# A cross-attention block on one core: V chains and encoder rows moved between units, a layer norm ahead of a V chain, and the last residual rows behind the last exchange

## The chip, the core and the metric

The kernel runs on one core of a Trainium2 chip. A core has TensorE (matmuls; the profile calls it PE, and its weight loads PEld), VectorE (DVE), ScalarE (ACT), GpSimd (POOL) and SyncE (SP), which here only issues transfers (DMAs). Each engine works through its own instructions in order, and waits for others by semaphores. The metric is the time of one execution on the device in microseconds (us); less is better. Everything is float32.

## What is computed

For each of four batches, with 512 query rows `x` and 512 encoder rows, 16 heads of 32 and a hidden width of 2048:

```python
residual = hidden_states
x = layer_norm(hidden_states, ln1_w, ln1_b)
q = (x @ q_w + q_b)      # then split into 16 heads
k = (encoder_hidden_states @ k_w + k_b)
v = (encoder_hidden_states @ v_w + v_b)
scores = jnp.einsum('bhqd,bhkd->bhqk', q, k) * scale
scores = jnp.where(mask, scores, mask_value)
attn = jax.nn.softmax(scores, axis=-1)
out = jnp.einsum('bhqk,bhkd->bhqd', attn, v)
hidden = out @ cproj_w + cproj_b + residual
y = layer_norm(hidden, ln2_w, ln2_b)
y = jax.nn.gelu(y @ fc_w + fc_b, approximate=True)
return hidden + y @ proj_w + proj_b
```

## The kernel before

**Groups and units.** The 16 heads of a batch are cut into four groups of four heads (128 columns), so that there are 16 groups `w` in all, four for each batch. A group has four units, one for each tile of 128 query rows. Unit `u = 4 w + qt` runs from 0 to 63. The texts call the columns of group `w` "K w", "Q w" and "V w": three chains of matmuls, `prep_k` (L230), `prep_q` (L240) and `prep_v` (L251). K and V read the batch's encoder rows `eT`, Q reads the normalized and transposed rows `xT`; both lie in one buffer, `xe`, one batch at a time. When a chain is done, ACT takes it out of PSUM, and the weights of two groups on (`load_w(w + 2)`) are loaded into the place of the weights just used. V's bias is added by POOL (`v_bias`, L267).

**One unit** is the loop body near L876. `scores` (L272): four matmuls into one PSUM tile with four banks (one buffer, so the next unit's scores wait until DVE has read it); for each head DVE adds the mask and takes the minimum (L284), ACT takes the exponential and its sum (L288). `turn` (L292): DVE transposes 32 by 32 blocks (L302) into a buffer `tb` that two units share. After the second, the reciprocals of the sums are added (L307 to L311), and a **pair** is formed: pair `p = 2 w + half`, formed in unit `2 p + 1`. `exchange` and `copies` (L320, L331) then move the pair's blocks between partitions with 16 DMAs (L345) of 136 KB on SP's queue. Pairs 1, 3, 5 and 7 go to `gt`, pairs 25 to 31 (odd ones) to `xe`, the others to the one buffer `pT`, which must have been read before.

**The attend.** `attend` (L348) multiplies a pair's blocks with V (32 matmuls, L362), and DVE scales the result into `oT` (L367). It stands at the head of a unit, before that unit's scores. Which unit is told by the table `AT` (L66) and, for units that aren't in it, by the rule "unit minus `LAG` (4), halved": pair 7 is attended in unit 18 before the change, pair 6 in 17, pair 8 in 20, pair 29 in 63.

**What else a unit does** is written by hand in the lists `first[w]` and `later[w]` (L790 to L866). A tuple in `first[w]` names the work of each of the four units; a list is spread over them by costs (`CHAIN` 3.4 and so on). This work follows the unit's scores and turn. It holds the chains of later groups (`A(w)`), the inputs of the next batch (`inputs(b)`: load of `x`; `x2`, the layer norm's two statistics parts and its application; `x3`, four turns by TensorE of that norm into `xT`; `x4`, the load of the encoder rows), output chains (`C(b)`, `cproj`, L399), and parts of the MLP (`some(n)` takes the next n of `mlp`). Layer norm 2 of a batch is `stat` (DVE, L145 and L146), `rs` (POOL, L151 and L153), `norm` (DVE, L167), and `turns2` (four turns by TensorE, L176, taken out by ACT and DVE, L181 and L179). `proj_bias` and `c_bias` add a row to four tiles on POOL (L374). All small accumulators share a ring of four PSUM banks (`ps_acc`), in order of use.

**The end.** For the last batch, `load_h` (L380) loads `x` again as the residual into places of K and Q that are free by then, and `c_bias` adds the output bias; `cproj` of that batch needs them, after the last attend. After the loop come the rest of the MLP's first part, the two last attends, the last output chains and `last_mlps`.

All these loads and exchanges go through SP's queue, in the order in which the program issues them.

Of the kernel before, what the change touches and what calls it, by code (L numbers as in the profile page):

```python
# [46 lines left out]
B, L, D, H = 4, 512, 512, 16  # L47
HD = D // H
INNER = 4 * D
NT = L // P  # L50
# [12 lines left out]
IN_G = (1, 3, 5, 7)  # L63
IN_XE = (25, 27, 29, 31)

AT = {u: (u - 5) // 2 for u in (5, 7, 9, 11, 13, 15, 17, 53, 55, 57, 59, 61, 63)}  # L66
BY_ACT = ((1, 1),)
MW = 8
WARM = 9
# [8 lines left out]
def xattn_block(ctx: ExitStack, tc: tile.TileContext, x, encT, mask, q_w, k_w, v_w, c_w, fc_w, p_w, vecs, rows, out):  # L78
# [36 lines left out]
    def k_q(w, i):  # L115
        n = w % 4 * 2 + i
        return pbt[:, n * D : (n + 1) * D]
# [19 lines left out]
    def acc_tile(name):  # L137
        return ps_acc.tile([P, D], F32, tag="acc", name=name)
# [9 lines left out]
    def ln_rs(key):  # L148

        ve = small.tile([P, NT], F32, tag="ve", name=f"ve{key[0]}_{key[1]}")  # L150
        nc.gpsimd.tensor_scalar(ve, S["mv", key][:, :, 1], EPS, 1.0, ALU.add, ALU.mult)  # L151
        rs = small.tile([P, NT], F32, tag="rs", name=f"rs{key[0]}_{key[1]}")
        nc.gpsimd.tensor_tensor(rs, ve, nhalf, ALU.pow)  # L153
        S["rs", key] = rs
        if key in BY_ACT:
            nm = small.tile([P, NT], F32, tag="nm", name=f"nm{key[0]}_{key[1]}")
            nc.gpsimd.tensor_tensor(nm, S["mv", key][:, :, 0], rs, ALU.mult)
            nc.gpsimd.tensor_scalar(nm, nm, -1.0, 0.0, ALU.mult, ALU.add)
            S["nm", key] = nm
# [24 lines left out]
    def queue(b):  # L184
        return Q[0] if b else nc.sync

    def load_enc(b):
        for d in range(ND):
            queue(b).dma_start(out=eT[:, d, :], in_=encT[b, ts(d, P), :])
# [30 lines left out]
    def load_w(w, queue=None, names=("wk", "wq", "wv")):  # L220

        if w >= NW:
            return
        g = w % NG
        for i, (n, src) in enumerate((("wk", k_w), ("wq", q_w), ("wv", v_w))):
            if n in names:
                S[n, w] = kqv_w(w, i)
                (queue or Q[0]).dma_start(out=S[n, w], in_=src[:, g, :, :])
# [11 lines left out]
    def prep_q(w):  # L240
        b, g = divmod(w, NG)
        qT = k_q(w, 1)
        acc = acc_tile(f"accq_{w}")
        for d in range(ND):
            nc.tensor.matmul(acc, S["wq", w][:, d, :], xT[:, d, :], start=(d == 0), stop=(d == ND - 1))  # L245
        load_w(w + 2, names=("wq",))

        nc.scalar.activation(qT, acc, AF.Identity, bias=qb[:, g : g + 1], scale=-scale)
        S["qT", w] = qT

    def prep_v(w):  # L251
        b = w // NG
        v = five.tile([P, NT, P], F32, tag="v", name=f"v_{w}")
        acc = acc_tile(f"accv_{w}")
        for t in range(NT):
            for d in range(ND):
                nc.tensor.matmul(  # L257
                    acc[:, ts(t, P)], eT[:, d, ts(t, P)], S["wv", w][:, d, :],
                    start=(d == 0), stop=(d == ND - 1),
                )  # L260
        load_w(w + 2, names=("wv",))
        nc.scalar.copy(v, acc.rearrange("p (t f) -> p t f", t=NT))  # L262
        S["v", w] = v
        if w:
            v_bias(w)

    def v_bias(w):  # L267
        v, bias = S["v", w], row[:, 2, ts(w % NG, P)]
        nc.gpsimd.tensor_tensor(v, v, bias[:, None, :].broadcast_to([P, NT, P]), ALU.add)  # L269
# [103 lines left out]
    def add_row(h, i):  # L373
        nc.gpsimd.tensor_tensor(h, h, row[:, i, :], ALU.add)  # L374

    def stays(b, t):

        return b == 0 or b == SPLIT and t < 2

    def load_h(b, *ts_):  # L380

        if ("xa", b) not in S:
            S["xa", b] = dram.tile([L, D], F32, tag=f"xa{b}", name=f"xa{b}")
        for t in ts_:
            if b == B - 1:

                S["h", b, t] = k_q(t // 2, t % 2)
            else:
                pool, tag = (hids, "hid") if stays(b, t) else (tiles, "xn")
                S["h", b, t] = pool.tile([P, D], F32, tag=tag, name=f"h_{b}_{t}")  # L390
            Q[0].dma_start(out=S["h", b, t], in_=x[b, ts(t, P), :])
            if stays(b, t):
                S["hid", b, t] = S["h", b, t]

    def c_bias(b):
        for t in range(NT):
            add_row(S["h", b, t], 0)
# [16 lines left out]
    def load_hid(b, ts_):  # L414

        for t in ts_:
            if ("hid", b, t) not in S:
                S["hid", b, t] = hids.tile([P, D], F32, tag="hid", name=f"hid_{b}_{t}")
            Q[0].dma_start(out=S["hid", b, t], in_=S["xa", b][ts(t, P), :])
        for t in ts_:  # L420
            add_row(S["hid", b, t], 1)

    def stat2(b, t):
        ln_stat((2, b), t, S["h", b, t])

    def norm2(b, t):
        h = S["h", b, t]
        y = tiles.tile([P, D], F32, tag="xn", name=f"xn2_{b}_{t}") if stays(b, t) else h
        S.setdefault(("yn", b), {})[t] = y
        ln_norm((2, b), t, y, h)  # L430

    def proj_bias(b):
        for t in range(NT):
            if stays(b, t):
                add_row(S["hid", b, t], 1)
# [276 lines left out]
    CHAIN, TURN = 3.4, 0.5  # L712

    def do(fn):
        return [(0.0, fn)]

    def A(w):
        if w >= NW:
            return []
        return [  # L720
            (CHAIN, lambda: prep_k(w)),
            (CHAIN, lambda: prep_q(w)),
            (CHAIN, lambda: prep_v(w)),
        ]

    def C(b):
        return [(CHAIN, lambda t=t: cproj(b, t)) for t in range(NT)]
# [4 lines left out]
    def turns2(b):  # L732
        return [(TURN, lambda d=d: ln2_turn(b, d)) for d in range(ND)]
# [7 lines left out]
    def inputs(b):  # L741
        ln = [(0.0, lambda part=part: ln1(b, part)) for part in range(3)]
        return do(lambda: load_x(b)), ln, turns1(b), do(lambda: load_enc(b))

    def run(work, budget=None):

        spent = 0.0
        while work and (budget is None or spent + work[0][0] / 2 <= budget):
            cost, fn = work.pop(0)
            fn()  # L750
            spent += cost
        return spent
# [27 lines left out]
    x1, x2, x3, x4 = inputs(1)  # L780
# [9 lines left out]
    first = [[] for _ in range(NW)]  # L790
    later = [[] for _ in range(NW)]
    k2, q2, v2 = A(2)
    k3, q3, v3 = A(3)
    k4, q4, v4 = A(4)
    k5, q5, v5 = A(5)
    k6, q6, v6 = A(6)
    first[0] = [(CHAIN, lambda: prep_v(1))], [(CHAIN, lambda: prep_q(1)), k2] + x2[:1], [k3] + x2[1:2], [v2]
    first[1] = [(CHAIN, lambda: (prep_v(3), load_enc(1)))] + x2[2:], [q2], [q3], x3[:2]
    first[2] = [k4], x3[2:] + [v4], [q4], [k5]
    first[3] = [q5], [v5], [k6, q6], [v6] + do(lambda: c_bias(0))  # L800
    mlp = []
    for p in range(SPLIT):
        mlp += FC(p, 0) + FC(p, 1) + PJ(p, 0) + FC(p, 2) + PJ(p, 1) + FC(p, 3) + PJ(p, 2) + PJ(p, 3)
# [2 lines left out]
    def some(n):  # L806
        taken, mlp[:n] = mlp[:n], []
        return taken

    def hid_(b, *ts_):  # L810
        return do(lambda: load_hid(b, ts_))

    def h_(b, *ts_):
        return do(lambda: load_h(b, *ts_))

    def cb(b):
        return do(lambda: c_bias(b))

    def pb_(b):
        return do(lambda: proj_bias(b))  # L820

    def rs(b):
        return do(lambda: ln_rs((2, b)))

    def stat(b, *ts_):
        return do(lambda: [stat2(b, t) for t in ts_])

    def norm(b, *ts_):
        return do(lambda: [norm2(b, t) for t in ts_])


    x1, x2, x3, x4 = inputs(2)
    k, q, v = A(7)
    c, t2 = C(0), turns2(0)
    first[4] = x1 + [k, q, v] + x4
    later[4] = c[:1] + x2[:1] + c[1:2] + x2[1:2] + c[2:3] + x2[2:] + c[3:]
    k, q, v = A(8)
    first[5] = (
        [k, v] + stat(0, 0, 1, 2, 3) + rs(0) + x3 + norm(0, 0, 1, 2, 3), [q] + t2 + pb_(0), some(2), some(2)
    )  # L840
    k, q, v = A(9)
    x1, x2, x3, x4 = inputs(3)
    first[6] = [k, q] + some(4) + [v] + x1
    k, q, v = A(10)
    first[7] = [k, q] + x2[:1] + some(2) + x2[1:2] + some(3) + [v]

    k, q, v = A(11)
    first[8] = h_(1, 0, 1) + x2[2:] + [k, q] + x3[:2] + some(1) + x3[2:] + [v] + h_(1, 2, 3) + x4
    later[8] = cb(1) + C(1)
    k, q, v = A(12)  # L850
    first[9] = [q] + some(2) + [k] + some(2) + [v]
    k, q, v = A(13)
    first[10] = [k, q] + some(4) + [v]
    k, q, v = A(14)
    t2 = turns2(1)
# [5 lines left out]
    k, q, v = A(15)  # L861
    c = C(2)
    first[12] = [k, q], cb(2) + [v], c[:2], c[2:]
    first[13] = some(1), some(1) + stat(2, 0, 1), some(1) + stat(2, 2, 3) + rs(2), some(2)
    first[14] = some(1) + norm(2, 0, 1), some(1) + norm(2, 2, 3), some(2) + h_(B - 1, *range(NT)), some(1)
    first[15] = hid_(1, 2, 3) + some(1), some(1), some(1) + cb(B - 1), some(2)  # L866

    for w in range(NW):
        if w and w % NG == 0:
# [6 lines left out]
        for qt in range(NT):  # L876
            u = w * NT + qt
            pair = AT.get(u, (u - LAG) // 2 if u >= LAG and u % 2 == 0 else None)
            if pair in AT.values() and u not in AT:
                pair = None  # L880
# [16 lines left out]
    exchange()  # L897

    first_c = FIRST * FQ // 2
    run(some(2))  # L900
    attend(NW - 1, 0)
    run(some(2))
# [57 lines left out]
```

## Time and profile before

| | |
|---|---|
| median of 3 runs | 817.76 us (816.22 to 820.13) |
| profiled execution | 823.1 us |
| its span | 821.3 us |
| PE busy | 796.2 us (97%), 4082 matmuls |
| DVE busy | 557.9 us (68%) |
| ACT busy | 355.5 us (43%) |
| POOL busy | 97.4 us (12%) |
| SP's queue | 59472 packets, 132.43 MB, 60.3% of 16 engines' span |
| chain of waits | PE 81%, DVE 7%, SP's queue 6%, DMA 4%, issue 1% |

Busy time and the chain are of one execution, taken by the hardware profiler. PE's busy time has modelled ends and says little on how full the array is; its idle time, and the clock that TensorE is granted, say more. In the lines of the profile "L345 SPq DMA_DIRECT2D pT<-tb x16" is sixteen issues by SP from line 345, from the tile `tb` into `pT`; the two numbers ahead of it are the start from the span's begin and the time from the first start to the last end, in us; in brackets stands the engine's idle time just before, and what ended it.

Scores start on PE at 35.5 us for unit 2, 40.2 (unit 3), 46.0 (4), 52.5 (5), 57.2 (6), 63.7 (7), 67.5 (8), 81.5 (9), 87.1 (10), 93.7 (11), 98.4 (12), 142.6 (18), 160.7 (20), 170.8 (21), 186.4 (22), 510.9 (62) and 521.5 (63). The stages after the last exchange, from 558 us on, are output chains and MLPs, with PE busy throughout.

### The profile page before, as it was taken

Reading aid. Unit: us, or ns where it says so; the run is one execution under the profiler, and the core shown is the slowest. Engines: PE = TensorE matmul, PEld = TensorE weight load, DVE = VectorE, ACT = ScalarE, POOL = GpSimd, SP = SyncE. Lnnn points to the kernel's source line nnn. Section 1 sums busy time; section 2 is a strip of 40 time slices with the busy share of each in tenths; the row PEclk is TensorE's granted clock in tenths of the full one; section 3 lists DMA queues with packets and bytes.
Section 4 is the critical chain, followed back from the end, with each engine's and each line's share of the span. In section 5 each row is a group of like instructions: output and inputs, shape, how many; then the busy total and the mean of one; then the engine's idle time right before and its main releaser. Section 6 shows DMA issues by size and latency. Waiting matters only on the chain.

```text
span 821.3 us, 11916 instructions
## 1 busy us (share of the span) xinstructions
PE 796.2 (97%) x4082; PEld 483.6 (59%) x4082; DVE 557.9 (68%) x1279; ACT 355.5 (43%) x779; POOL 97.4 (12%) x110
## 2 busy tenths in 40 slices
PE   9996999979999999999999999899999999999998
PEld 6452555454454554545553433345888888888887
DVE  3796877985677767667788998625737984258511
ACT  2674655346673645547654469700311331023200
POOL 1120003030000011000131000300031012200011
PEclk9998999989999999999999999999999999999999
DMA  9888988856797868688667799964334430023001
GB/s 329 280 206 238 230 220 223 215 134 160 174 241 172 221 174 239 149 211 205 156 161 207 189 269 241 234 193 131 88 129 135 148 115 14 26 77 89 2 14 38
DMA packets 60956, 137.14 MB, mean 167 GB/s; under 512 B 12464, under 2 KB 15664, under 8 KB 60768
## 3 DMA queue, kind: packets, MB, share of 16 engines
q1 hardware_dynamic: 59472, 132.43, 60.3%
q0 software_dynamic: 896, 2.82, 1.1%
q10 hardware_dynamic: 528, 1.14, 0.6%
q8 instruction: 32, 0.52, 0.3%
q14 instruction: 28, 0.23, 0.1%
HBM read 58.22 MB, written 6.82 MB: 79 GB/s over the span
## 4 chain that ended last, share of the span: by engine, by line
PE 81%; DVE 7%; SPq 6%; DMA 4%; issue 1%; ACT 0%; POOL 0%; DVEq 0%; POOLq 0%
PE q L573 15%; PE accp L479 8%; PE accf L469 7%; PE accc L403 7%; PE sc L279 6%; PE av L362 6%; SPq L345 6%; PE acck L235 6%; PE accq L245 5%; PE accv L257 5%; DVE ptt L284 3%; PE q5p L613 2%; PE q3p L613 2%; PE q7p L613 2%; PE q2p L613 2%; PE q1p L613 2%
## 5 line engine op out<-in xcount | busy, mean ns | idle before, releaser
L288 ACT ACTIVATE ptt<-ptt,mn 128x512 f32<-128x512 f32 x256 | 181.6, 711 | 145.0 <-DVE mn L284 144.9
L284 DVE CUSTOM_DVE_ANT_0 ptt<-sc,mb 128x512 f32<-128x512 f32 x256 | 161.0, 684 | 45.1 <-PE sc L279 44.9
L302 DVE STREAM_TRANSPOSE tb<-ptt 128x512 f32<-128x512 f32 x224 | 141.9, 683 | 9.6 <-DMA pT<-tb 5.2
L469 PE MATMUL accf<-yT,pbt 128*128 128x512 f32 x192 | 87.3, 601 | 0.0
L479 PE MATMUL accp<-pbt,gt 128*128 128x512 f32 x192 | 86.2, 599 | 0.0
L279 PE MATMUL sc<-pbt 32*128 32x512 f32 x512 | 73.5, 644 | 4.0 <-DVE mn L284 3.2
L573 PE MATMUL q<-ys,gt 128*128 128x256 f32 x320 | 75.1, 379 | 0.0
L573 PEld LDWEIGHTS q<-ys,gt 128*128 128x128 f32 x320 | 60.8, 190 | 8.3
L469 PEld LDWEIGHTS accf<-yT,pbt 128*128 128x128 f32 x192 | 35.0, 190 | 50.4 <-issue 45.4
L257 PEld LDWEIGHTS accv<-ptt,xe 128*128 128x128 f32 x512 | 58.9, 192 | 9.7 <-issue 7.2
L479 PEld LDWEIGHTS accp<-pbt,gt 128*128 128x128 f32 x192 | 35.3, 190 | 48.4 <-issue 46.5
L257 PE MATMUL accv<-ptt,xe 128*128 128x128 f32 x512 | 60.6, 277 | 1.3 <-DVE xe L179 1.3
L235 PE MATMUL acck<-xe,ptt 128*128 128x512 f32 x128 | 59.4, 607 | 0.0
L573 PE MATMUL q<-yT,gt 128*128 128x256 f32 x240 | 58.1, 379 | 0.5 <-DVE gt L501 0.5
L245 PE MATMUL accq<-xe,ptt 128*128 128x512 f32 x128 | 58.3, 598 | 0.0
L403 PE MATMUL accc<-wc,oT 128*128 128x512 f32 x128 | 56.7, 597 | 0.0
L362 PE MATMUL av<-pT,v 128*32 128x256 f32 x768 | 49.8, 403 | 6.5 <-DMA pT<-tb 6.5
L269 POOL TENSOR_TENSOR v<-v,row 128x512 f32<-128x512 f32 x16 | 20.5, 1282 | 291.1 <-ACT v L262 291.1
L577 ACT ACTIVATE ga<-uc,vec 128x256 f32<-128x256 f32 x40 | 20.3, 508 | 75.8 <-DVE uc L551 75.8
L573 PEld LDWEIGHTS q<-yT,gt 128*128 128x128 f32 x240 | 45.5, 190 | 7.4 <-DVE gt L501 0.9
L584 ACT COPY p<-q 128x256 f32<-128x256 f32 x20 | 7.1, 353 | 95.0 <-PE q L573 95.0
L288 ACT ACTIVATION_READ_ACCUMULATOR ptt<-ptt,mn 128x1 f32 x256 | 47.9, 187 | 0.0
(121 smaller groups left out, 939.9 us busy)
## 6 DMA issues: line engine op xcount, KB each, us to landing
pT<-tb SPq DMA_DIRECT2D x384, 136.0 KB, 2.4
pbt<-p_w_dram SPq DMA_DIRECT2D x40, 256.0 KB, 3.0
gt<-fc_w_dram SPq DMA_DIRECT2D x40, 256.0 KB, 2.7
gt<-tb SPq DMA_DIRECT2D x64, 136.0 KB, 2.5
xe<-tb SPq DMA_DIRECT2D x56, 136.0 KB, 3.2
pbt<-fc_w_dram SPq DMA_DIRECT2D x24, 256.0 KB, 4.0
ptt<-k_w_dram SPq DMA_DIRECT2D x16, 256.0 KB, 3.5
xe<-encT_dram SPq DMA_DIRECT2D x16, 256.0 KB, 4.4
```

The costliest lines, as they stand in the source:

```text
L235: nc.tensor.matmul(acc, S["wk", w][:, d, :], eT[:, d, :], start=(d == 0), stop=(d == ND - 1))
L245: nc.tensor.matmul(acc, S["wq", w][:, d, :], xT[:, d, :], start=(d == 0), stop=(d == ND - 1))
L257: nc.tensor.matmul(acc[:, ts(t, P)], eT[:, d, ts(t, P)], S["wv", w][:, d, :], start=(d == 0), stop=(d == ND - 1),)
L279: nc.tensor.matmul(sc[:, h, :], qT[r, ts(qt, P)], kT[r, :], start=True, stop=True)
L284: nc.vector.tensor_tensor_reduce(out=s, in0=sc[:, h, :], in1=S["mb", w // NG], scale=1.0, scalar=FMAX, op0=ALU.add, op1=ALU.min, accum_out=mn,
L288: nc.scalar.activation(s, s, AF.Exp, bias=mn, scale=-1.0, accum_out=sums[:, qt, h : h + 1])
L302: nc.vector.transpose(tv[:, q, h], S["ps", w, qt][h])
L362: nc.tensor.matmul(av[ts(h, HD), : 2 * P].rearrange(shape, **kw), v[:, t, ts(h, HD)], p[t][h], start=(t == 0), stop=(t == NT - 1),)
L403: nc.tensor.matmul(acc, S["oT", b][:, g, ts(t, P)], wc[:, g, :], start=(g == 0), stop=(g == NG - 1))
L469: nc.tensor.matmul(acc, S["fcw", b, f][:, d, :], S["yT", b][:, d, :], start=(d == 0), stop=(d == ND - 1))
L479: nc.tensor.matmul(acc, gT[q % 2][:, k, ts(t, P)], S["pw", b, q * FQ + k], start=(k == 0), stop=(k == FQ - 1))
L573: nc.tensor.matmul(o, a[:, k], y[:, k], start=(k == 0), stop=(k == 1))
```

## The change

The order in which the program issues its work is changed in four places; no instruction is added or left out.

1. In the first batch's groups (units 2 to 15) V 2 moves from unit 3 to 2; V 3 and the load of the second batch's encoder rows from unit 4 to 3; Q 2 and Q 3 each one unit earlier; K 4 from unit 8 to 6; V 4 from 9 to 8, with the last two turns of the second batch, and Q 4, K 5 and V 5 one or two units earlier, K 6 and Q 6 into units of their own.
2. Pair 7 is attended in unit 19 instead of 18 (`AT`).
3. In group 5, unit 20 does K 8, the statistics, root and application of layer norm 2 of batch 0 and the turns of batch 2's inputs; V 8 moves behind them to unit 21, ahead of Q 8. `proj_bias` of batch 0 moves from unit 21 to the end of unit 22.
4. The load of the last batch's residual rows moves from unit 58, and its `c_bias` from unit 62, to behind the exchange that follows the loop.

```diff
-AT = {u: (u - 5) // 2 for u in (5, 7, 9, 11, 13, 15, 17, 53, 55, 57, 59, 61, 63)}
+AT = {u: (u - 5) // 2 for u in (5, 7, 9, 11, 13, 15, 17, 19, 53, 55, 57, 59, 61, 63)}
...
-    first[0] = [(CHAIN, lambda: prep_v(1))], [(CHAIN, lambda: prep_q(1)), k2] + x2[:1], [k3] + x2[1:2], [v2]
-    first[1] = [(CHAIN, lambda: (prep_v(3), load_enc(1)))] + x2[2:], [q2], [q3], x3[:2]
-    first[2] = [k4], x3[2:] + [v4], [q4], [k5]
-    first[3] = [q5], [v5], [k6, q6], [v6] + do(lambda: c_bias(0))
+    first[0] = (
+        [(CHAIN, lambda: prep_v(1))], [(CHAIN, lambda: prep_q(1)), k2] + x2[:1], [k3, v2] + x2[1:2],
+        [(CHAIN, lambda: (prep_v(3), load_enc(1)))]
+    )
+    first[1] = [q2] + x2[2:], [q3], [k4], x3[:2]
+    first[2] = x3[2:] + [v4], [q4], [k5], [v5]
+    first[3] = [q5], [k6], [q6], [v6] + do(lambda: c_bias(0))
...
     first[5] = (
-        [k, v] + stat(0, 0, 1, 2, 3) + rs(0) + x3 + norm(0, 0, 1, 2, 3), [q] + t2 + pb_(0), some(2), some(2)
+        [k] + stat(0, 0, 1, 2, 3) + rs(0) + x3 + norm(0, 0, 1, 2, 3), [v, q] + t2, some(2) + pb_(0), some(2)
     )
...
-    first[14] = some(1) + norm(2, 0, 1), some(1) + norm(2, 2, 3), some(2) + h_(B - 1, *range(NT)), some(1)
-    first[15] = hid_(1, 2, 3) + some(1), some(1), some(1) + cb(B - 1), some(2)
+    first[14] = some(1) + norm(2, 0, 1), some(1) + norm(2, 2, 3), some(2), some(1)
+    first[15] = hid_(1, 2, 3) + some(1), some(1), some(1), some(2)
...
     exchange()
 
     first_c = FIRST * FQ // 2
+    load_h(B - 1, *range(NT))
+    c_bias(B - 1)
     run(some(2))
     attend(NW - 1, 0)
```

## The prediction

> **What bounds the kernel.** The page first: TensorE is busy 97% of the span, the chain of waits is 81% PE, so only its idle and its slow stretches can be won. The waits of PE alone name them:
>
> ```profile
> PE av L362 <- DMA pT<-tb: 6.5, 3, 5.6
> PE tp L176 <- ACT pbt L248: 4.2, 1, 4.2
> ...
> PE av L362 <- DMA xe<-tb: 2.5, 1, 2.5
> PE av L362 <- ACT rr L309: 1.2, 1, 1.2
> ```
>
> (us in total, times, longest.) Four places hold 13.5 us of about 20 us of idle. The table by stretches of 10 us adds the granted clock:
>
> ```profile
> 70.00:80.00 10.00, 4.40 (x26) 1.89 (x28) 4.82 (x13) 4.54 (x11) 0.00 (x0) 0.73 0.82 212
> ...
> 180.00:190.00 10.00, 8.22 (x49) 3.65 (x50) 5.41 (x15) 3.67 (x7) 0.00 (x0) 0.66 0.19 42
> ```
>
> The first number after the length is PE's busy time, the third last the clock: 0.73 and 0.66, where it is 1.00 elsewhere. Then the timeline, at each place:
>
> ```profile
> 60.25 1.86 SPq L189 DMA_DIRECT2D xe<-encT_dram  x4
> 62.22 13.76 SPq L345 DMA_DIRECT2D pT<-tb  x16
> 77.90 3.64 PE L362 MATMUL av<-pT,v 128*32 128x256 f32 x32 [5.60 <-DMA pT<-tb]
> ...
> 140.74 1.93 PE L362 MATMUL av<-gt,v 128*32 128x256 f32 x32 [1.17 <-ACT rr L309]
> ...
> 169.83 1.30 POOL L269 TENSOR_TENSOR v<-v,row 128x512 f32<-128x512 f32 x1 [15.22 <-ACT v L262]
> 172.55 3.82 DVE L167 TENSOR_SCALAR xn<-h,mv,rs 128x512 f32<-128x512 f32 x4 [1.03 <-POOL rs L153]
> 173.17 5.55 POOL L374 TENSOR_TENSOR h<-h,row 128x512 f32<-128x512 f32 x4 [0.66 <-DVE xn L167]
> 181.78 1.12 PE L176 MATMUL tp<-ident,xn 128*128 128x128 f32 x4 [4.15 <-ACT pbt L248]
> ...
> 501.12 1.80 SPq L391 DMA_DIRECT2D pbt<-x_dram  x4
> 503.03 13.08 SPq L345 DMA_DIRECT2D xe<-tb  x16
> 518.12 3.43 PE L362 MATMUL av<-xe,v 128*32 128x256 f32 x32 [2.49 <-DMA xe<-tb]
> ```
>
> The same 32 attention products take 1.9 us at 140.74 and 3.6 and 3.4 after the gaps: the slow clock costs another 1.8 and 1.6 us. An undisturbed exchange is 16 issues of 0.635 us, 10.2 us, and lands 2.4 us after its last; the two in front of gaps took 13.8 and 13.1. Why, the landings tell: the issues of pair 2 resume at 66.42, 67.86 and 70.39, just after encoder rows land at 66.40, 67.84 and 70.37. [...]
>
> **Part 1: units 2 to 15 (V 2, V 3, encoder rows, K 4).** Nothing is added or removed; four weight loads change places in SP's queue (V 4 ahead of pair 1, Q 4 ahead of pair 2). I follow it from scores to scores, with the rows of the chain and timeline: scores hold PE 1.07, a K or Q chain 3.63 (3.43 behind another), V 3.77 (3.57), an attend 1.86, half a turn 1.03; DVE begins 1.21 after the scores start, frees their bank 2.45 later, and needs 2.4 more (even unit) or 2.8 (odd) to form the pair.
>
> - Unit 2: scores 35.5, K 3, now V 2 too, so scores 3 start at 43.7, not 40.2. DVE had been busy until 43.1, so pair 1 is formed 1.9 later, at 50.2 against 48.3. It issues to 60.4 (the V 4 load has gone ahead, at about 45.8, where SP stood idle until 48.45).
> - Then V 5 and the encoder rows, at 61.1 to 62.5 (were 60.25 to 61.68). One weight instead of two lies ahead, worth the 1.2 between the landings of the two; by before's delays (4.4 for the first row, 8.7 for the last) the rows land from 64.3 to 70.0. They are no earlier than before.
> - PE: scores 4 at 48.6, Q 2, attend 0, scores 5 at 55.1, Q 3, scores 6 at 59.8 to 60.9. Now K 4 stands next, **ahead of attend 1 and scores 7**, and waits for the rows: idle 60.9 to 64.3, then as the rows come, done at 71.0. That is a new stall, in place of the one removed; the half clock in it is hidden by the rows.
> - Attend 1, scores 7 at 72.9, turns, scores 8 at 76.6 (DVE), turns and V 4 to 82.3. Pair 2 restarts with the last row at 70.0, nine issues more to 75.8, landed 78.2: attend 2 finds it. Scores 9 at 84.2, Q 4, scores 10, K 5, attend 3 (pair 3 formed 79.4, landed 92) at 93.5, scores 11, V 5, scores 12 at 100.2.
>
> Before, scores 12 start at 98.48 without V 5 (3.77): 102.25 on equal work. **Gain 2.0.** From there the order differs by a chain and no exchange is late (pair 5 lands 114.5, attend 116.2). If the rows land as late as on before's schedule plus the 0.9 of later issue, 71.3, it is 0.7; with two more us of crowding −1.3. At best the rows come with their median delay, 6.2: 68.7, gain 3.3.
>
> **Part 2: attend of pair 7 from unit 18 to 19.** Pair 7's last transfer lands at 140.54, and PE stood 1.17 for it. Now scores 18 (bank free at 138.3) and two output chains (7.07) come first; these read the first half of the rows only. Gain 1.2; if pair 7 came 8 us later still nothing. Bounds 0 and 1.2.
>
> **Part 3: unit 20 and 21.** On POOL, V's bias (1.30) stood ahead of the layer norm's root; now the root goes when the statistics end (170.05): 171.3, not 172.5. The four norms follow DVE's evacuations at 171.55. They took 3.82 beside POOL's row additions, 1.90 at 158.94 without; these additions are now two units later, under fc: norms done 173.5, not 176.4. Scores 21's reduction 173.5 to 176.0, the exponents to 177.1, then ACT's queue: copy of rr to 178.3, V 8's evacuation 178.9, Q 8's 179.5. PE: K 8, turns, scores 21 (167.2), V 8, Q 8 to 175.5, two turns to 176.4. The third turn needs V 8's bank (four banks in the ring): 178.9, the last 180.0. Attend 9 at 180.0 instead of 182.8. So 2.5 us of idle are left, late is ACT, and the question is the clock. [...] I take **2.7**, the row of the same length; 4.5 is the other end.
>
> **Part 4: last x.** The four loads left SP ahead of pair 29. Pair 29 is formed at 501.4; without them it issues 501.5 to 511.7 and lands 513.5. PE comes at 515.6. The gap and the slow attend go: 2.49 + (3.43 − 1.86) = **4.1**; what follows is free: scores 63 need DVE at 516.9, PE is there at 517.5. The loads now follow pair 31 on SP, issued by about 541, landed by 546; POOL's four additions (1.25 each, 4.96) end by 551; DVE first reads these rows at 561.5 − 4. Cover 6 us. Pair 31 isn't behind them. Bounds 2.5 (clock drops all the same) and 4.1.
>
> **Sum.** 2.0 + 1.2 + 2.7 + 4.1 = 10.0 us of the profiled execution: 823.1 (span 821.3 and 1.8 around it) to 813.1. That execution was 5.3 above the median of the runs, 817.76; the same gain from it gives **807.8**. All parts at the low bounds (−1.3 + 0 + 2.7 + 2.5) gain 3.9: 813.9. At the high ones 13.1: 804.7.
>
> **Rivals.** (a) *The first group gives back what it takes:* DVE and SP are nearly full there (DVE 9.9 of 10 us from 40 to 60, SP's exchanges follow one another to 123 us), so V 2 early delays pair 1, and a K 4 that ends at 77 instead of 71 makes part 1 a loss of 4: 817.8 + 4 − 8.0 = 813.8. For it: encoder rows are no sooner. Against: before idles 5.6 at the same rows and has V 4 still to do. (b) *The gains are caught by the next wait:* the remaining gaps (1.3 at 289, 0.6 at 428, 0.9 at 484) grow as PE comes sooner. These waits belong to the local chain of their unit, which moves along; only part 4 and one us per place would stay, about 6: 812. (c) *Slower:* K 4 blocks the in-order PE for as long as a whole exchange. If the rows came only with pair 2 or behind it, the last would land at about 84 and K 4 end at 85: part 1 loses 12, the sum is +4, **822**. It decides from 10 us of lateness (K 4 past 81, since the three other parts hold 8.0). Against: SP's order puts the rows ahead of pair 2, and before its rows landed ahead of it in that order. (d) *That it doesn't do what it says:* encoder rows that only move with V 3 are issued no earlier at all, which is so; the profit is V 4 in the gap, and is in the sum.
>
> **How the numbers follow.** Forecast 0.66 (own range 803.5 to 811.5), (a) 0.14, (b) 0.10, (c) 0.07, something unseen 0.03. The range, 803 to 814, takes in the bounds and (a) and (b). A measurement of this kernel can tell 0.5%, 4.1 us, from no change: faster is below 813.7. The forecast is that, (b) mostly and half of (a): 0.83; within 0.09; slower 0.08.
>
> **What would show it.** Right: K 4 (L235) in unit 6 waits for the encoder's DMA, some 3 to 5 us near 61, and no attend waits near 78; no PE wait at 141; the norms (L167 from h) take 1.9 and the wait for L248 becomes about 2.5; pair 29's issues take 10.2, and the attend near 510 takes 1.9. Wrong: a PE wait over 8 us near 61, a granted clock under 0.6 in that stretch, or new waits of attends on pT between 85 and 135.

## The result, and the profile after

The changed kernel takes **812.77 us** (median of 10 runs, 811.88 to 814.23), the kernel before, run beside it, 817.78 (815.92 to 822.08). The ratio is 0.9935, with a 95% interval of 0.9923 to 0.9948: faster by 5 us. The profiled execution took 812.55 us (span 810.8). So the two profiled executions lie 10.5 us apart, as the sum had it (10.0), but the medians only half of that. This gap is the main question of what follows.

The page of the changed kernel, busy times and the chain of waits:

```profile
PE 793.0 (98%) x4082; PEld 481.7 (59%) x4082; DVE 556.2 (69%) x1279; ACT 355.6 (44%) x779; POOL 98.0 (12%) x110
...
PE 86%; DVE 5%; SPq 5%; DMA 2%; issue 1%; ACT 0%; POOL 0%; DVEq 0%; POOLq 0%
```

The chain has moved from the transfers (DMA 4% to 2%, SP's queue 6% to 5%) to PE. PE's waits in the same execution (us in total, times, longest):

```profile
PE acck L235 <- DMA xe<-encT_dram: 4.2, 1, 4.2
PE sc L279 <- DVE mn L284: 2.5, 2, 1.6
PE tp L176 <- ACT v L262: 2.3, 1, 2.3
...
PE accv L257 <- ACT xe L181: 0.8, 1, 0.8
PE av L362 <- DMA pT<-tb: 0.8, 2, 0.5
```

The waits for pairs (6.5 and 2.5) are down to 0.8, and those for pair 7's reciprocals (1.2) and for Q 8's evacuation (4.2) are gone. New at the head is K 4's wait for encoder rows. The table by stretches shows what the clock did (PE's busy time stands after the length, the granted clock third last):

```profile
60.00:70.00 10.00, 5.75 (x14) 2.13 (x7) 6.24 (x16) 3.92 (x10) 0.00 (x0) 0.70 0.94 264
70.00:80.00 10.00, 7.64 (x67) 3.61 (x65) 5.91 (x16) 4.64 (x12) 0.00 (x0) 0.96 0.81 205
170.00:180.00 10.00, 7.72 (x59) 4.60 (x61) 8.75 (x21) 5.86 (x13) 2.72 (x4) 1.00 0.49 136
```

Before has three slow stretches, behind its gaps near 75, 180 and 518 us (the prediction reads the clock as 1.00 outside the first two; before's row from 510 to 520 us has 0.92). The last two are gone, and the first now lies ten us earlier, where PE waits for rows. The timeline at the four places:

```profile
64.95 6.57 PE L235 MATMUL acck<-xe,ptt 128*128 128x512 f32 x8 [4.25 <-DMA xe<-encT_dram]
71.44 1.93 PE L362 MATMUL av<-gt,v 128*32 128x256 f32 x32
77.10 1.14 PE L279 MATMUL sc<-pbt 32*128 32x512 f32 x8 [1.63 <-DVE mn L284]
80.11 3.84 PE L257 MATMUL accv<-ptt,xe 128*128 128x128 f32 x32 [0.84 <-ACT xe L181]
83.88 1.93 PE L362 MATMUL av<-pT,v 128*32 128x256 f32 x32
...
170.08 1.91 DVE L167 TENSOR_SCALAR xn<-h,mv,rs 128x512 f32<-128x512 f32 x4
177.31 1.25 PE L176 MATMUL tp<-ident,xn 128*128 128x128 f32 x8 [2.28 <-ACT v L262]
178.48 1.93 PE L362 MATMUL av<-pT,v 128*32 128x256 f32 x32
...
494.98 10.19 SPq L345 DMA_DIRECT2D xe<-tb  x16
509.04 1.93 PE L362 MATMUL av<-xe,v 128*32 128x256 f32 x32
```

Step by step this is what the prediction drew: K 4 ends at 71.4 (71.0 was forecast), attend 2 finds its pair, the norms take 1.91, PE waits 2.28 for V 8's evacuation, pair 29's sixteen issues take 10.2 us and its attend runs at full clock. In one point it differs: after the wait of 2.28 the clock did not fall, and attend 9 took 1.93.

**Where the time lies**, from scores to scores, in the profiled execution of each kernel (PE's timeline, starts of scores subtracted; * marks a kernel with the part that bears on the row; e1 to e5 are the experiments below, e1 being before once more):

| stretch (us) | before | e1 | e2 | e3 | e4 | after | e5 |
|---|---|---|---|---|---|---|---|
| scores 0 to 16 (part 1) | 102.16 | 101.13 | 101.35* | 101.71 | 101.43 | 102.32* | 99.78 |
| scores 17 to 20 (part 2) | 26.08 | 25.99 | 25.51 | 26.13 | 25.32 | 24.84* | 24.84* |
| scores 20 to 23 (part 3) | 34.22 | 33.01 | 34.10 | 29.12* | 33.51 | 29.12* | 29.12* |
| scores 62 to 63 (part 4) | 10.62 | 8.02 | 6.64 | 7.15 | 6.57* | 6.56* | 6.57* |

With the change the last three rows are the same to 0.01 us in these executions. (Of the later runs, e6 takes 30.54 in the third row, since its clock fell there (0.91 from 170 to 190 us), and e11 26.18 in the second, with a wait of 1.27 for a pair.) Without it they scatter, and before's own profiled execution was the longest or nearly so in all of them. Against it, the parts are worth −0.2, 1.2, 5.1 and 4.1: 10.2 us. Against the mean of the other executions without the part they are worth −0.8 (102.32 and 101.35 against the mean of e1, e3, e4 and e5), 0.9, 4.4 and 0.7: **5.2 us**, which is what the medians show. Each entry is one execution, so this is a reading, not a measurement. Two later runs show how wide it is: e7, which has part 1, takes 100.67 us in the first row, and e8, which lacks part 2, 24.84 in the second; with them these two parts are worth −0.4 and 0.7. The experiments test the parts one by one.

### The profile page after: what moved, and what is told of

It reads as the page before. It is cut to its first block, busy times and chain, and to the rows that moved or that the text cites. A ratio compares the mean times of both kernels' runs of the same rounds, so it can differ in the third digit from the quotient of the medians.

```text
span 810.8 us, 11911 instructions
## 1 busy us (share of the span) xinstructions
PE 793.0 (98%) x4082; PEld 481.7 (59%) x4082; DVE 556.2 (69%) x1279; ACT 355.6 (44%) x779; POOL 98.0 (12%) x110
## 4 chain that ended last, share of the span: by engine, by line
PE 86%; DVE 5%; SPq 5%; DMA 2%; issue 1%; ACT 0%; POOL 0%; DVEq 0%; POOLq 0%
PE q L573 15%; PE accf L469 9%; PE accp L479 8%; PE accc L403 7%; PE sc L279 7%; PE av L362 7%; PE acck L235 6%; PE accv L257 6%; PE accq L245 6%; SPq L345 5%; PE q5p L613 2%; PE q3p L613 2%; PE q7p L613 2%; PE q6p L613 2%; PE q1p L613 2%; PE q2p L613 2%
## 5 line engine op out<-in xcount | busy, mean ns | idle before, releaser
L235 PE MATMUL acck<-xe,ptt 128*128 128x512 f32 x128 | 62.0, 629 | 4.2 <-DMA xe<-encT_dram 4.2
L235 PEld LDWEIGHTS acck<-xe,ptt 128*128 128x128 f32 x128 | 24.5, 200 | 39.2 <-issue 31.5
L362 PE MATMUL av<-pT,v 128*32 128x256 f32 x768 | 46.4, 382 | 0.8 <-DMA pT<-tb 0.8
```

The lines of the kernel that those rows point to most:

```text
L235: nc.tensor.matmul(acc, S["wk", w][:, d, :], eT[:, d, :], start=(d == 0), stop=(d == ND - 1))
L362: nc.tensor.matmul(av[ts(h, HD), : 2 * P].rearrange(shape, **kw), v[:, t, ts(h, HD)], p[t][h], start=(t == 0), stop=(t == NT - 1),)
```

## The experiments

Ratios are to the kernel before, run beside each kernel on the same chip, with 95% intervals. 1 us is 0.0012. e1 to e4 share a chip, e5 to e8 another, e9 to e11 a third.

**e1: before, unchanged.** Is the profiled execution of before typical? In the expectations C is the theory that the granted clock differs from run to run and that runs with a lower clock are slower, T that the transfers differ.

> The kernel before, unchanged. Its profiled execution had a mean granted clock of 0.990 (three slow stretches after three gaps, 17 us in all) and took 823.1 us, 5.3 above its median; the changed kernel's runs have 0.995 or 0.996 and spread over 2.4 us only. [...] Rival T (transfers): the clock is alike in all runs (0.990 to 0.991) and the runs differ because transfers land at different times; then time and clock don't go together.

Measured: ratio 1.0002 (0.9986 to 1.0018), median 818.36. Its profiled execution took 817.9. The timeline of e1 at pair 2 and pair 29:

```profile
75.78 3.64 PE L362 MATMUL av<-pT,v 128*32 128x256 f32 x32 [3.83 <-DMA pT<-tb]
...
500.77 11.73 SPq L345 DMA_DIRECT2D xe<-tb  x16
514.55 1.93 PE L362 MATMUL av<-xe,v 128*32 128x256 f32 x32 [1.38 <-DMA xe<-tb]
```

The same waits were 5.60 and 2.49 in the execution that the prediction rests on; pair 29's issues took 13.08 there and 11.73 here, and after the shorter gap the clock did not fall (1.00 from 500 to 530 us, the attend at 1.93). Both explanations hold a part. The clock: in 29 runs of before the mean granted clock was 0.9934, in the profiled execution 0.990, and runs with more slow time are longer (819.9 us on average at a clock of 0.9925 or less, 817.0 at 0.995 or more). The slope over these runs is 0.35 us for each us of slow clock, and 0.990 has about 6 us more of it, so an estimated 2 of the 4.6 us between that execution and their median of 818.5. (This is a rough split: the clock was also down, at 0.50 from 74.67 to 81.49 us in before's profile, at the long wait of 5.60, so the slope holds some of both.) The rest is put down to transfers that land at other times: the wait for pair 2 was 3.83, 4.43, 3.90 and 3.62 in e1, e3, e4 and e5, where nothing about it is changed, never 5.60 again.

**e2, e3, e4: one part each.**

```diff
# e2_part1_only: before, with first[0] to first[3] of the change
# e3_part3_only: before, with
-        [k, v] + stat(0, 0, 1, 2, 3) + rs(0) + x3 + norm(0, 0, 1, 2, 3), [q] + t2 + pb_(0), some(2), some(2)
+        [k] + stat(0, 0, 1, 2, 3) + rs(0) + x3 + norm(0, 0, 1, 2, 3), [v, q] + t2, some(2) + pb_(0), some(2)
# e4_part4_only: before, with load_h and c_bias of the last batch behind the last exchange
```

> Part 1 alone (units 2 to 15). By the two profiles part 1 gained 0 on equal work by unit 16: the wait for pair 2 (5.6 us and a slow attend) went, and K 4's wait for the encoder rows (4.3 us, at the slow clock to its end), two waits on DVE and ACT (1.6 and 0.8) came. Theory C: the old slow attend (1.8) was not paid in the median run, so here the median is 0 to 2 us slower than before, ratio 1.000 to 1.0025. The prediction's part 1 as written: 2.0 faster, ratio 0.9975. Rival T: 0, ratio 1.000.

> Part 3 alone (V 8 behind layer norm 2, row additions one unit later). By the two profiles it gained 5.1. Theory C: less in the median, where the slow clock after the old gap isn't paid always: 2.7 to 4.5, ratio 0.9945 to 0.9967. Rival T: the full 5.1, ratio 0.9938. In its profile the norms take 1.9 instead of 3.8 and the wait of the turns about 2.3.

> Part 4 alone (last residual rows behind the last exchange). By the two profiles it gained 4.06: the wait 2.49 and the slow attend 1.57. Theory C: 2.5 in a median run with no slow clock there, at most 4.1: ratio 0.995 to 0.997. Rival T: the encoder and residual rows' landing varies, and the gain is anything from 0 to 4.

| | ratio to before | us |
|---|---|---|
| e2, part 1 | 1.0017 (1.0001 to 1.0033) | 1.4 slower |
| e3, part 3 | 0.9956 (0.994 to 0.9972) | 3.6 faster |
| e4, part 4 | 0.9987 (0.9975 to 0.9998) | 1.1 faster |

Part 3 carries the change. Part 4 is worth a quarter of its forecast, since the wait that it removes is rarely as long as in the one profile. e2 has the old order at pair 29, and its timeline shows no wait there at all:

```profile
500.32 11.05 SPq L345 DMA_DIRECT2D xe<-tb  x16
...
513.64 1.93 PE L362 MATMUL av<-xe,v 128*32 128x256 f32 x32
```

Part 1, for which a gain of 2.0 was forecast, is a small loss. Part 2 was not run alone; with its 0.7 to 1.2 from the timelines the parts sum to 4.0 to 4.5 us, of 5 measured together.

**e5: the change without part 1.**

```diff
# after, with first[0] to first[3] as before
```

> The changed kernel with its units 2 to 15 as before (parts 2, 3 and 4 stay). Alone, part 1 measured 1.0017 of before (0.1 to 2.7 us slower). If the parts add up this kernel is 0.1 to 2.7 us faster than the changed one: ratio to before 0.990 to 0.9935, about 0.992, and its attend of pair 2 waits some 4 us near 76. Rival (the prediction's part 1: a gain of 2.0 that only a slow run hides): 0.996.

Measured: ratio 0.9923 (0.9903 to 0.9943), median 812.09, against 0.9935 for the change. That agrees with e2 in sign, but the intervals overlap; that part 1 costs something rests on e2, whose interval (from 1.0001) nearly takes in no loss, and on the first row of the table above. That it gains 2.0 us is out by both.

**e6: K 4 behind attend 1.** In the timeline of after, attend 1 and scores 7 stand behind K 4 and are ready long before its rows.

```diff
-    first[1] = [q2] + x2[2:], [q3], [k4], x3[:2]
+    first[1] = [q2] + x2[2:], [q3], [], x3[:2] + [k4]
```

> The changed kernel with K 4 moved from unit 6 to unit 7, behind attend 1 and the two turns. Theory K: part 1 loses because K 4's wait for the encoder rows stands ahead of attend 1 and scores 7 on the in-order PE, though these need nothing from it. Then scores 7 start at about 65 instead of 73, pair 3 is formed by 72 instead of 80, K 4 runs from about 67 to 71, and the stretch to unit 16 is 3 to 5 us shorter than in the changed kernel: ratio to before 0.988 to 0.990. Rival S: SP's queue bounds the stretch, exchange after exchange, and the gain is lost by unit 18: ratio 0.993.

Measured: ratio 0.9895 (0.9876 to 0.9915), median 809.89. The timeline of e6:

```profile
62.52 1.93 PE L362 MATMUL av<-gt,v 128*32 128x256 f32 x32 [1.76 <-DMA gt<-tb]
64.38 1.14 PE L279 MATMUL sc<-pbt 32*128 32x512 f32 x8
66.38 3.14 PE L235 MATMUL acck<-xe,ptt 128*128 128x512 f32 x6
69.78 1.13 PE L235 MATMUL acck<-xe,ptt 128*128 128x512 f32 x2 [0.25 <-DMA xe<-encT_dram]
...
78.68 1.93 PE L362 MATMUL av<-pT,v 128*32 128x256 f32 x32 [2.06 <-DMA pT<-tb]
```

Scores 7 start at 64.4 instead of 73.3, and by scores 16 4.0 us are kept against after, 2.4 against e7, which has the same order as after in these units. The rows come as late as in after, but one unit of other work now covers them. Two smaller waits are left, 1.76 for pair 1 and 2.06 for pair 2. On one chip the medians are 813.06 for e7, 812.09 for e5 (these units as before) and 809.89 for e6. So it was the place of K 4 in PE's order, not the early V chains, that took part 1's gain.

**e7: the row additions back beside the norms.** The prediction said that the norms halve because POOL's additions go away from beside them.

```diff
-        [k] + stat(0, 0, 1, 2, 3) + rs(0) + x3 + norm(0, 0, 1, 2, 3), [v, q] + t2, some(2) + pb_(0), some(2)
+        [k] + stat(0, 0, 1, 2, 3) + rs(0) + x3 + norm(0, 0, 1, 2, 3), [v, q] + t2 + pb_(0), some(2), some(2)
```

> The changed kernel with the four row additions of POOL left in unit 21 (V 8 stays behind the layer norm). Theory P: the norms were slow because DVE and POOL ran side by side; here POOL's additions start with the first norm again, the norms take 3.8 instead of 1.9, the exponents of unit 21, V 8's evacuation and the third turn come 1.9 later, the wait of the turns is about 4.2 and part 3 keeps only the 1.2 of the earlier root and what the moved V saves: 1.5 to 3.5 us slower than the changed kernel (a slow clock included), ratio to before 0.995 to 0.9975. Rival: only the order of V's bias and the root counted; the same as the changed kernel, 0.9935.

Measured: ratio 0.9933 (0.9916 to 0.9951), no different from the change. The timeline of e7:

```profile
169.76 1.92 DVE L167 TENSOR_SCALAR xn<-h,mv,rs 128x512 f32<-128x512 f32 x4
...
177.00 1.28 POOL L269 TENSOR_TENSOR v<-v,row 128x512 f32<-128x512 f32 x1 [7.28 <-ACT v L262]
178.25 4.96 POOL L374 TENSOR_TENSOR h<-h,row 128x512 f32<-128x512 f32 x4
```

The additions stand in POOL's queue behind V 8's bias, which waits for V 8's evacuation. Since V 8 itself has moved, they start at 178.25 wherever they are written; in the changed kernel it is 178.58. Moving `proj_bias` was worth nothing; moving V 8 took the additions along. Since they don't meet the norms here, e7 does not test whether they slow them. Before's trace shows that: of its four norms, the two that start ahead of the first addition take 0.55 and 0.54 us, and the two that run beside additions to their end 1.5 each.

**e8: what is a slow clock worth?** Thirteen matmuls into the attend's own bank, which the attend then overwrites, fill part of PE's wait for pair 2 in before.

```diff
+        for _ in range(13 if (w, half) == (1, 0) else 0):
+            nc.tensor.matmul(av[:, :P], ident, ident, start=True, stop=True)
```

> The kernel before with 13 small products of the identity ahead of the attend of pair 2, 3.0 us of PE work into the place that the attend overwrites; they fill part of the wait at 72 to 77 and need nothing that comes late. The stage's wait for the transfers stays. Theory C: the clock stays up, the attend takes 1.9 instead of 3.6, and the median falls by about 1.8: ratio 0.998. Rival: the slow clock there costs nothing because the next units wait for DVE or SP anyway: 1.000.

Measured: ratio 0.9971 (0.9955 to 0.9987), 2.4 us faster with more work. The timeline of e8:

```profile
71.70 3.06 PE L356 MATMUL av<-ident 128*128 128x128 f32 x26
...
76.47 1.93 PE L364 MATMUL av<-pT,v 128*32 128x256 f32 x32 [1.71 <-DMA pT<-tb]
```

The wait is cut in two, what is left is 1.71, and the attend takes 1.93 instead of 3.64. Those 1.7 us are what this gap cost beyond itself, and most of the 2.4 that the kernel gained (interval 1.1 to 3.7).

**e9: V 9 among the turns of unit 21.** Can the wait of 2.28 be filled as well? On top of e6:

```diff
-        [k] + stat(0, 0, 1, 2, 3) + rs(0) + x3 + norm(0, 0, 1, 2, 3), [v, q] + t2, some(2) + pb_(0), some(2)
+        [k] + stat(0, 0, 1, 2, 3) + rs(0) + x3 + norm(0, 0, 1, 2, 3), [v, q] + t2[:2],
+        t2[2:] + [A(9)[2]] + some(2) + pb_(0), some(2)
...
-    first[6] = [k, q] + some(4) + [v] + x1
+    first[6] = [k, q] + some(4) + x1
```

> K 4 behind attend 1, and the wait of the turns filled: turns 3 and 4 of layer norm 2 stand behind attend 9 and scores 22, and V 9 comes from group 6 between them and fc. Theory A (ACT's order sets that wait: V 8's evacuation stands behind the exponents): attend 9 starts at once, the wait of 2.3 us and the slow clock that sometimes follows go: 2.3 to 3.5 us faster than K 4 behind attend 1 alone, ratio to before 0.985 to 0.987. Rival: fc then waits for DVE's evacuation of the third turn, which stands behind a whole unit's work (2.5 us or more), and nothing is gained: 0.9895.

Measured: ratio 0.9868 (0.9841 to 0.9894). That lies where theory A put it, and its interval overlaps e6's; but V 9's move has no part in it. From scores 20 to scores 62, which hold all of it, e6's profile takes 346.04 us and e9's 346.37. The wait stays, under another name, as e9's timeline shows:

```profile
172.00 3.52 PE L362 MATMUL av<-pT,v 128*32 128x256 f32 x32 [2.29 <-ACT v L262]
```

Now it is attend 9 that takes the third place in the ring behind V 8 and Q 8, whose bank is V 8's own. Whatever comes there waits for V 8's evacuation; the turns were not the cause. Theory A is wrong.

**e10, e11: encoder rows ahead of pair 1.** In after SP stands idle from 47.3 to 50.0 us, works through pair 1 and issues the rows at 61.1. Here pair 1's exchange is put behind unit 3's other work, and so behind the rows. e11 adds the V 9 edit of e9.

```diff
-        if w < NW - 1 or half == 0:
+        if (w, half) != (0, 1) and (w < NW - 1 or half == 0):
             exchange()
...
                 run(work[qt])
+                if w == 0 and qt == 3:
+                    exchange()
```

> The changed kernel, with pair 1's exchange issued behind unit 3's work, so that V 5 and the encoder rows go ahead of it on SP's queue, which stands idle from 47 to 50. Theory Q (the rows' place in SP's queue is what costs: K 4 waits for them, and pair 2 behind them is held up by their late landing): the rows land by 56, K 4 finds them in unit 6, pair 1 lands by 65 to 66 (attend 1 waits 1 to 2 us), pair 2's issues take 10.2 instead of 12.9 and land by 76: 4 to 6 us faster than the changed kernel, ratio to before 0.986 to 0.989. Rival B (the transfers' bandwidth bounds the stretch, whatever the order): pair 1 and 2 land as late as before, 0.991 to 0.9935.

> The rows ahead of pair 1 and V 9 in the wait of the turns, both. If both theories hold and the gains add: ratio to before 0.982 to 0.986, about 805 us, and PE's waits in the first 300 us are below 6 us in all.

Measured: e10 0.9854 (0.9827 to 0.9882), median 807.52; e11 0.9851 (0.9826 to 0.9876), median 806.97. The timeline of e10, SP and PE:

```profile
48.65 2.14 SPq L189 DMA_DIRECT2D xe<-encT_dram  x4
50.90 12.22 SPq L345 DMA_DIRECT2D gt<-tb  x16
63.86 10.37 SPq L345 DMA_DIRECT2D pT<-tb  x16
...
60.52 3.70 PE L235 MATMUL acck<-xe,ptt 128*128 128x512 f32 x8
65.05 1.93 PE L362 MATMUL av<-gt,v 128*32 128x256 f32 x32 [0.84 <-DMA gt<-tb]
77.49 1.93 PE L362 MATMUL av<-pT,v 128*32 128x256 f32 x32
```

The rows go out 12 us sooner, mostly into time that SP had free. K 4 finds them. Pair 1 pays for it (12.22 us of issues instead of 10.36) and is late by 0.84 only; pair 2, no longer behind rows, issues in 10.37 us instead of 13.02. Scores 16 start 96.15 after scores 0, 6.2 sooner than in the changed kernel. This is the best version found: 1.5% below before and about 0.8% below the changed kernel, if the two ratios are set side by side. V 9 adds nothing to it either: e11's PE waits for 9.5 us in the first 300 us, where below 6 was expected.

## Why the prediction was right or wrong

**The forecast of 807.8 was 5.0 us too low**, though the range held the time. The step that failed is "the same gain from it gives 807.8": a gain of 10.0 us worked out on one execution was carried over whole to the median. The waits that the change removes were what made that execution slow, so its 5.3 us above the median were a part of the gain already: in the four rows of the table before lies 1.1, 0.3, 0.7 and 3.4 us above the mean of the other executions without the part, 5.5 in all. The size of a wait for a transfer was taken as a constant of the kernel; e1 to e5 showed that it isn't.

**Part 1 (2.0 forecast; a loss of 1.4 alone, interval 0.1 to 2.7).** The path was right: rows no sooner, a new stall of 4.25 at K 4, K 4 done at 71.4 (71.0 forecast), pair 2 in time. That K 4 ended so near the forecast is luck. Its last row landed at 69.05, a us sooner than forecast, but the half clock was not hidden by the rows, as the prediction had it: K 4 took 6.57 us, most of it at a clock of 0.50 (from 63.95 to 70.78 us), and ended 2.5 after that row. In e6, at full clock (1.00 from 50 to 90 us), K 4 ended 1.2 after its last row, so the clock cost an estimated 1.3. Scores 12 start 1.7 us later than forecast (101.85 against 100.2): 0.4 of it is K 4's end, and 0.84 was missed, since V 4 waits for a bank of the ring while ACT evacuates the turns only behind the exponents. The rest is the base: the stall that part 1 removes, 5.60 in the profile, was 3.62 to 4.43 in the other executions that have it. Rival (a), that the first group gives back what it takes, is nearest to what happened, though not for its reason: pair 1 issues from 50.03 instead of 48.45, as forecast, which attend 1 doesn't feel, but K 4 stood ahead of ready work, which is the mechanism of rival (c) at a tenth of its size. e6 shows this.

**Part 2 (1.2).** 1.24 in the two profiles, 0.7 to 0.9 against the other executions. The wait is gone, as forecast, but it too varies: e8, without the part, has none at pair 7. Not run alone.

**Part 3 (2.7, other end 4.5; measured 3.6 alone, interval 2.3 to 4.9, and 4.4 to 5.1 in the timelines).** The order, the wait left over (2.5 forecast, 2.28 measured) and what is late next (V 8's evacuation on ACT) were right. Mis-sized was the clock. The row of before (slow after 2.49) was taken; in after the clock stayed up. No run shows the 2.7 itself, or the 4.5: in their place stand the 3.6 and the 4.4 to 5.1. One row was too little to go by. The same wait of 2.28 or 2.29 stands at this place in after, e3, e5, e6, e7, e9 and e10. In five of them the attend that comes next takes 1.93 us; in e6 it takes 2.63, in e9 3.52. The stretch from 170 to 190 us in after, e3, e6 and e9:

```profile
170.00:190.00 20.00, 17.72 (x96) 8.48 (x95) 14.42 (x35) 12.15 (x25) 6.26 (x6) 1.00 0.63 155
170.00:190.00 20.00, 17.72 (x102) 9.37 (x104) 15.30 (x35) 10.98 (x24) 7.37 (x7) 1.00 0.64 156
170.00:190.00 20.00, 17.72 (x88) 8.53 (x87) 13.00 (x32) 13.36 (x28) 6.19 (x5) 0.91 0.57 130
170.00:190.00 20.00, 18.00 (x106) 9.98 (x107) 9.45 (x23) 10.41 (x20) 7.45 (x6) 0.91 0.60 141
```

In the first three PE is busy for the same 17.72 us, and the clock is 1.00, 1.00 and 0.91. What decides is not shown, so neither end of the forecast could be counted on. e6's fall cost 1.42 us in the third row of the table (30.54 against 29.12). With a fall in 2 of 7 executions, as here, an estimated 0.4 us of the 4.4 goes (1.42 × 2 / 7), which leaves 4.0; 3.6 was measured, with 4.0 inside its interval.

The reason given for the shorter norms was half wrong: the additions did cost them 1.9 us, but it was V 8's move that took them away (e7), not the edit of `proj_bias`.

**Part 4 (4.1, bounds 2.5 to 4.1; 1.1 alone, interval 0.2 to 2.0).** All of the mechanism came as forecast: 10.19 us of issues, no wait, the attend at 1.93, the loads hidden behind pair 31. In the two profiles it gave 4.06. The term that was mis-sized is the wait itself, 2.49 with a slow attend in the one execution, and 1.38, 0 and 0.51 with a fast one in e1, e2 and e3 (e3's profile puts the 0.51 down to ACT's L470, for which the same attend doesn't wait in after). Even the low bound lay above the truth, since it varied the clock but not the wait.

**The other rivals.** (b), that later waits catch the gains, would have given 812, close to the result, for a wrong reason: from scores 23 to scores 62 the profiles of before and after take 315.91 and 315.86 us, so nothing was caught. (d) did not arise.

## What to carry to other kernels

A wait for a transfer in one profiled execution is one draw. Before its length is counted as a gain, set that execution's time and granted clock against the median run, and profile the same kernel a second time: what both show can be won. A chain whose data come late belongs behind the work that is ready, also when that costs it a unit (e6 is 1.05% faster than before, the change 0.65%); still better, its load goes where the queue is idle (e10).

## What the runs showed of the hardware

- **The granted clock was down at PE's longer gaps, and a gap of 2.28 us did not always lower it.** In before's profile it was 0.50 from 74.67 to 81.49, from 180.48 to 187.31 and from 518.40 to 521.81 us, at gaps of 5.60, 4.15 and 2.49. Gaps of 2.28 or 2.29 at one place were followed by an attend of 1.93 us in five profiles and of 2.63 and 3.52 in two. Behind gaps of 3.62 to 5.60, ahead of pair 2's attend in before, e1, e3, e4 and e5, the attend took 3.25 to 3.64 us instead of 1.93 each time. Work of no use in the gap (e8) made the kernel 0.3% faster.
- **With shorter waits the time scattered less.** Before, with gaps of 5.60, 4.15 and 2.49 us on its path in the profile, has runs from 815.92 to 822.08; the changed kernel, with gaps of 4.25 and 2.28, from 811.88 to 814.23. That the gaps are the cause was not tested.
- **Transfers with the same order and the same sizes land at different times.** Pair 29's sixteen issues took 13.08, 11.73 and 11.05 us in before, e1 and e2, and 10.19 where no loads stood ahead. What makes the difference from run to run stays open; it was not tried.
